# Attention inside a fused four-layer kernel: projections moved to a block's first step, closing weight sums behind them, one addition for four heads

## The chip, the cores and the metric

The kernel runs on one core of a Trainium2 chip. The metric is the device time of one execution in microseconds; the time given for a kernel is the median over several executions. All data are fp32.

## What is computed

Four layers run in a row on x, 16 images of 384 channels and 16x16 points, seen as two sequences of N = 2048 tokens. The change touches only the first, an attention with 12 heads of 32 dimensions whose values are the input itself:

```
qk   = (xt @ qk_w.T)                          # q and k, 12 heads of 32
attn = softmax(q * 32**-0.5 @ k.T)
attn = alpha * eye + beta * attn - gamma / N
out  = attn @ v                               # v = xt
```

The other three are a ConvNeXt block (7x7 depthwise convolution, norm over channels, 384 to 1536 to 384, with a global response norm between the two products), a Sobel block (two fixed 3x3 filters, a 768 to 384 product, norm, gelu, residual) and a block with two 1x1 convolutions round a 3x3 depthwise one, a linear attention, and a norm with an MLP of 384 to 1536 to 384.

## The kernel before, in words

**Attention.** There are six units (2 sequences times 3 groups of four heads). A unit has 4 blocks of 512 queries, a block 16 steps of 128 keys; 24 blocks and 384 steps in all. A step `t` of block `n` issues, in this order:

- `scores(n, t)`: four score products, one for each head, on TensorE (`st` in the profile) into two PSUM tiles, each two banks wide, of a pool of three; then two exponentials on ScalarE, each 128x1024 (two heads), into two `e` tiles in SBUF (a pool of eight, so four steps deep).
- `weighted` of the step before: four products with the values (`av`), added up over the block in one PSUM bank, and on VectorE the running sum of the `e` tiles, in two additions of 128x1024 (`s`). After `ADDS[n]` steps such a sum ends and a new one begins: the list has 4, 8, 16 or 2 for each of the 24 blocks.
- A finished sum is added up over the partitions by TensorE with a matrix of ones (`weights`, `dn` in the profile). A sum that ends inside the block does so in four quarters of 128 columns in later steps; the one that ends the block in one piece of 512 columns, two steps later. Then `finish` copies the result to SBUF (`r`), and VectorE inverts it in four pieces, scales the `av` sum with it (copied before to `va` by ScalarE, beside `xg`, the part with `alpha` and `gamma`) and writes the layer's output, one piece in each following step.
- In step `SLOT` = 5 of a block, `project` makes two of the coming q or k tiles: 12 matmul instructions (`p`) into the third PSUM tile, two copies on ScalarE, and on the way a load of v by SyncE's queue. There are projections in blocks 0 to 21 (a single one in block 21).
- `fill` puts work of the second layer into the step: taps of the 7x7 convolution on VectorE (`y`), and, from block 20 on, the norms of its first tiles (the leads). How much comes from `pace`, a table of what a step takes on TensorE and on VectorE.

The three engines' instructions are pinned to this program order. A dictionary `due` holds what is to be issued in which step.

**Everything after attention** is laid out by a list scheduler (`Plan`), which takes, of the operations that can start within `SLACK`, that of the task with the lowest rank. `TURNS` is the order of the 16 MLPs (0 for the second layer, 1 for the fourth; one weight set is loaded for each entry), `RANK` the ranks, `AFTER` the point from which convolution outputs may use buffers of another pool. Only the first two convolution tiles may be made during attention.

A group's line in the profile is always L96, a helper that records every instruction, so the tiles' names tell what is meant.

Of the kernel before, what the change touches and what calls it, by code (L numbers as in the profile page):

```python
# [9 lines left out]
F32 = mybir.dt.float32  # L10
AF = mybir.ActivationFunctionType
ALU = mybir.AluOpType
# [3 lines left out]
P = 128  # L16
C = 384
NC = C // P
NB = 2
# [4 lines left out]
HD = 32  # L24
# [3 lines left out]
BLK = 512  # L28
NBLK = N // BLK
NIP = NBLK  # L30
NQC = N // P
SLOT = 5
LEAD = 20 * NQC + 6
FIRST = NQC + 10

TURNS = (
    (0, ((0, 0), (0, 1), (0, 2), (0, 3),)),
    (1, ((0, 0), (0, 1),)),
    (0, ((1, 0), (1, 2),)),
    (1, ((0, 2),)),  # L40
    (0, ((1, 1), (1, 3),)),
    (1, ((1, 0), (0, 3), (1, 2), (1, 1), (1, 3),)),
)
AFTER = ('x4', 0, 2)

RANK = {
    "mid": ((36.6, 22.0, 24.3, 85.6), (18.6, 42.9, 96.6, 26.9)),
    "l1": ((50.1, 89.5, 75.2, 4.0), (51.1, 16.8, 81.7, 28.5)),
    "l3c": ((45.7, 99.2, 100.9, 121.0), (-20.9, -6.3, 70.9, 62.0)),
    "conv": 109.4,  # L50
}
SLACK = 0.196
JUNK = 2

ADDS = (16, 8, 16, 16, 4, 4, 4, 2, 2, 8, 16, 16, 4, 16, 2, 4, 16, 8, 4, 4, 4, 4, 4, 4)
XB, YB, SB = 12, 2, 22
TB = BLK // P
RB = 2 * HW
# [135 lines left out]
def pace(t):  # L194


    n, i = divmod(t - 1, NQC)
    adds = ADDS[n]
    pe, dve = 2.066, 2.275 if t and i % adds else 0.0
    at = i - adds - 1  # L200
    parts = sum(j * adds // 4 == at % adds for j in range(4)) if at >= 0 else 0
    if parts:
        pe += 0.22 * parts
    elif i == 1 and n > 0:
        pe += 0.87
    else:
        pe += 0.09
    if n > 0:
        dve += {2: 0.88, 3: 0.88, 4: 0.88, 5: 0.88, 6: 0.6, 7: 0.66}.get(i, 0.0)
    return pe, dve  # L210


# [185 lines left out]
def attention(tc, X, xt, L0, block, small, col, cols, ones, load_qk, banks, fill, bound):  # L398
# [6 lines left out]
    with ExitStack() as actx:  # L405
        pool = lambda name, bufs, **kw: actx.enter_context(tc.tile_pool(name=name, bufs=bufs, **kw))
        wqk_sb = pool("wqp", 1).tile([P, NC, 2, NC, P], F32, name="wqk_sb")
        load_qk(wqk_sb)
        ep = pool("ep", 8)
        sp = pool("sp", 4)  # L410
        op = pool("op", 2)
        pst = pool("pst", 3, space=PSUM)
        pacc = pool("pacc", 1, space=PSUM)
# [37 lines left out]
            return made, early, late  # L451


        due = {}

        def unit(u, made, gm):

            b, g = units[u]
            q, keys, v = made["q"], made["k"], made["v"]
            adds = ADDS[u * NBLK : (u + 1) * NBLK]  # L460
            acc, sums = {}, {}

            def scores(n, t):
                es = []
                for i in range(2):
                    es.append(ep.tile([P, 2, BLK], F32, tag="e", name=f"e_{u}_{n}_{t}_{i}"))
                sts = [bank2(f"st_{u}_{n}_{t}_{i}") for i in range(2)]
                for h in range(4):
                    rows = slice(HD * h, HD * (h + 1))
                    pe.matmul(  # L470
                        sts[h // 2][:, h % 2, :],
                        keys[t // TB][rows, ts(t % TB, P)],
                        q[n][rows, :],
                        start=True,
                        stop=True,
                    )
                for i in range(2):
                    act.activation(es[i], sts[i], AF.Exp, scale=HD**-0.5)
                return es

            def weighted(n, t, es):
                if t == 0:
                    acc["av"] = pacc.tile([P, BLK], F32, tag="av", name=f"av_{u}_{n}")
                for h in range(4):
                    pe.matmul(
                        acc["av"][HD * h : HD * (h + 1), :],
                        v[t // TB][:, (t % TB) * P + HD * h : (t % TB) * P + HD * (h + 1)],
                        es[h // 2][:, h % 2, :],
                        start=(t == 0),
                        stop=(t == NQC - 1),  # L490
                    )
                at = t % adds[n]
                for i in range(2):
                    if at == 0:
                        sums[i] = es[i]
                    elif at == 1:
                        s = sp.tile([P, 2, BLK], F32, tag="s", name=f"s_{u}_{n}_{t}_{i}")
                        dve.tensor_tensor(s, sums[i], es[i], ALU.add)
                        sums[i] = s
                    else:  # L500
                        dve.tensor_tensor(sums[i], sums[i], es[i], ALU.add)


                k = (u * NBLK + n) * NQC + t
                if at == adds[n] - 1:
                    parts = 1 if t == NQC - 1 else 4
                    for i in range(parts):
                        due.setdefault(k + 2 + i * adds[n] // 4, []).append(
                            lambda i=i, summed=dict(sums): weights(
                                n, t, summed, ts(i, BLK // parts)  # L510
                            )
                        )
                for f in due.pop(k, ()):
                    f()
                if t == NQC - 1:
                    va = op.tile([P, BLK], F32, tag="va", name=f"va_{u}_{n}")
                    act.activation(va, acc["av"], AF.Copy, scale=1.0)
                    xg = op.tile([P, BLK], F32, tag="xg", name=f"xg_{u}_{n}")
                    act.activation(
                        xg, X[b][n][:, g, :], AF.Identity, scale=col("alpha", g), bias=gm  # L520
                    )
                    due[k + 2].append(lambda: finish(n, va, xg))

            def weights(n, t, summed, at):
                if t == adds[n] - 1 and at.start == 0:
                    acc["dn"] = pacc.tile([P, BLK], F32, tag="dn", name=f"dn_{u}_{n}")
                for h in range(4):
                    pe.matmul(
                        acc["dn"][HD * h : HD * (h + 1), at],
                        ones[:, :HD],  # L530
                        summed[h // 2][:, h % 2, at],
                        start=(t == adds[n] - 1 and at.start == 0),
                        stop=(t == NQC - 1),
                    )

            def finish(n, va, xg):

                if g == 0:
                    L0[b][n] = block(f"l0_{b}_{n}")
                k = u * NBLK + n  # L540
                r = op.tile([P, BLK], F32, tag="r", name=f"r_{u}_{n}")
                act.activation(r, acc["dn"], AF.Identity, accum_out=bound[:, 0, k : k + 1])

                def invert(i):
                    dve.reciprocal(r[:, ts(i, P)], r[:, ts(i, P)])

                def scale():
                    dve.tensor_tensor(va, va, r, ALU.mult)

                def check():  # L550
                    junk = op.tile([P, BLK], F32, tag="junk", name=f"junk_{u}_{n}", bufs=1)
                    act.activation(junk, r, AF.Identity, accum_out=bound[:, 1, k : k + 1])

                def put():
                    dve.scalar_tensor_tensor(
                        L0[b][n][:, g, :], va, col("beta", g), xg, ALU.mult, ALU.add
                    )

                todo = [*(lambda i=i: invert(i) for i in range(TB)), scale, put]
                for i, f in [*enumerate(todo), (8, check)]:  # L560
                    due.setdefault((k + 1) * NQC + 2 + i, []).append(f)

            return scores, weighted

# [14 lines left out]
        for u, (b, g) in enumerate(units):  # L579
            steps = late_steps  # L580
            scores, weighted = unit(u, made, means[b][0][:, g : g + 1])
            if u + 1 < len(units):
                made, early, late_steps = projections(*units[u + 1])
                steps = steps + early
            for n in range(NBLK):
                for t in range(NQC):
                    es = scores(n, t)
                    added = 0.0
                    if before:
                        before()  # L590
                    before = lambda f=weighted, a=(n, t, es): f(*a)
                    if t == SLOT and steps:
                        added = project(f"p_{u}_{n}", steps[:2])
                        del steps[:2]
                    fill((u * NBLK + n) * NQC + t, added)
            assert not steps
        before()
# [7 lines left out]
def conv_seq_kernel(  # L605
# [869 lines left out]
    if fast:  # L1475
# [5 lines left out]
        def fill(t, added=0.0):  # L1481
# [12 lines left out]
            for task in (*leads, conv):  # L1494
# [3 lines left out]
                while task is not conv or ("y", 0, YB - 1, NC - 1) not in plan.made:  # L1498
                    op = task.head
# [1 line left out]
                        task.rest = t + 1 + (before.engine == "DVE")  # L1501
                        break
                    if op.engine == "DVE":
                        if free < max(0.4, op.length - 1.5):
                            break
                        free -= op.length + 0.12 * (before in op.after)
                    if not plan.holds(task, "wa") or not plan.step(task):
# [144 lines left out]
```

## Time and profile before

| what | value |
|---|---|
| median of 3 runs | 2674.13 us (2673.81 to 2677.04) |
| profiled execution | 2679.38 us, its span 2677.6 us |
| attention in it, first score product to the last step | 22.1 to about 1048.5 us |
| TensorE busy | 2644.6 us, 99% of the span |
| VectorE busy | 2011.5 us, 75% |
| ScalarE busy | 1557.5 us, 58% |
| DMA | 55.69 MB, 21 GB/s on average |

The profiled execution is 5.25 us longer than the median, and has 1.8 us outside its span. In the groups a row gives line, engine, operation, output and inputs, their shapes, the count, busy time and mean duration, and idle time before it with what ended it. PE is TensorE, DVE VectorE, ACT ScalarE. One matmul of the source is two instructions in the profile, so a step's four score products are eight `st` instructions. Ends of matmuls are modelled and overlap the next; the distance between starts is what a step really takes.

### The profile page before, as it was taken

To read this page: it belongs to the slowest core of one execution; us is meant where nothing else is said; L and a number is where in the kernel's file an instruction comes from. 1 tells how busy PE (TensorE), PEld (TensorE's weight loads), DVE (VectorE), ACT (ScalarE), POOL (GpSimd) and SP (SyncE) were. 2 spreads that over 40 slices of the span, in tenths; PEclk is the share of its full clock that TensorE was granted. 3 is DMA by queue.
4 is the path that set the end of the run, shared out by engine and by line. 5 is a ranking of instruction groups with operands and counts; after the bars stand their busy time and mean duration, and the time that the engine had idled before them with its cause. 6 is when DMAs were issued, how large, how long until landed. Compare 5 with 4: busy or idle time off the path is not lost. (4 is left out here: it accounts for less than half of the span.)

```text
span 2677.6 us, 32803 instructions
## 1 busy us (share of the span) xinstructions
PE 2644.6 (99%) x12997; PEld 1061.5 (40%) x12997; DVE 2011.5 (75%) x2588; ACT 1557.5 (58%) x2314; POOL 7.4 (0%) x54
## 2 busy tenths in 40 slices
PE   8999999999999999899999999999999999999999
PEld 2223333233323323345444454444444444454443
DVE  5999999999999889999999999999652202732300
ACT  6787878878787888564565335457443542625201
POOL 0000000000000000000000000000000000000000
PEclk9999999999999999999999999999999999999999
DMA  3000000000000003000001001011001110000000
GB/s 150 5 13 1 9 9 5 13 1 5 13 1 1 1 13 108 23 0 0 1 1 47 25 12 31 29 36 36 24 24 36 47 36 24 0 1 1 12 17 20
DMA packets 28851, 55.69 MB, mean 21 GB/s; under 512 B 1680, under 2 KB 14096, under 8 KB 28688
## 3 DMA queue, kind: packets, MB, share of 16 engines
q1 hardware_dynamic: 28544, 53.35, 6.0%
q8 instruction: 104, 1.70, 0.3%
q14 instruction: 59, 0.48, 0.1%
q10 hardware_dynamic: 144, 0.15, 0.0%
HBM read 47.21 MB, written 6.29 MB: 20 GB/s over the span
## 5 line engine op out<-in xcount | busy, mean ns | idle before, releaser
L96 ACT ACTIVATE e<-st 128x1024 f32<-128x1024 f32 x768 | 743.2, 1025 | 88.5 <-PE st L96 80.7
L96 DVE SCALAR_TENSOR_TENSOR y<-l,vec,y 128x420 f32<-128x420 f32 (+8 forms) x1152 | 660.0, 638 | 5.0
L96 DVE TENSOR_TENSOR s<-s,e 128x1024 f32<-128x1024 f32 x444 | 513.3, 1216 | 11.7 <-ACT e L96 11.2
L96 PE MATMUL st<-q,k 32*128 32x512 f32 x3072 | 474.1, 641 | 4.0 <-ACT e L96 2.3
L96 PE MATMUL av<-e,v 128*32 128x512 f32 x3072 | 410.9, 606 | 4.3 <-ACT va L96 4.2
L96 PE MATMUL ph_l<-y,wa 128*128 128x512 f32 x576 | 261.4, 597 | 0.0
L96 PE MATMUL ph_l3c<-d_l3c,wa 128*128 128x512 f32 x576 | 258.4, 593 | 0.0
L96 PE MATMUL po_l<-hid_l,wb 128*128 128x512 f32 x576 | 255.7, 596 | 1.1 <-ACT hid_l L96 1.1
L96 PE MATMUL po_l3c<-hid_l3c,wb 128*128 128x512 f32 x576 | 256.6, 593 | 0.0
L96 PEld LDWEIGHTS st<-q,k 32*128 32x128 f32 x3072 | 146.1, 183 | 220.1 <-issue 132.4
L96 DVE TENSOR_TENSOR s<-e,e 128x1024 f32<-128x1024 f32 x162 | 191.0, 1221 | 54.7 <-ACT e L96 36.0
L96 ACT ACTIVATE hid_l<-ph_l,vec 128x512 f32<-128x512 f32 x96 | 66.0, 687 | 202.9 <-PE ph_l L96 202.8
L96 ACT ACTIVATE hid_l3c<-ph_l3c,vec 128x512 f32<-128x512 f32 x96 | 65.6, 687 | 202.6 <-PE ph_l3c L96 202.5
L96 PEld LDWEIGHTS av<-e,v 128*32 128x32 f32 x3072 | 60.6, 108 | 298.1 <-issue 274.0
L96 DVE SCALAR_TENSOR_TENSOR o_l3c<-po_l3c,vec,l 128x512 f32<-128x512 f32 x24 | 17.5, 748 | 209.6 <-PE po_l3c L96 208.8
L96 PEld LDWEIGHTS po_l<-hid_l,wb 128*128 128x128 f32 x576 | 109.5, 191 | 139.1 <-issue 128.0
L96 PEld LDWEIGHTS ph_l3c<-d_l3c,wa 128*128 128x128 f32 x576 | 108.8, 190 | 137.2 <-issue 133.4
L96 PEld LDWEIGHTS ph_l<-y,wa 128*128 128x128 f32 x576 | 109.1, 191 | 136.0 <-issue 125.1
L96 PEld LDWEIGHTS po_l3c<-hid_l3c,wb 128*128 128x128 f32 x576 | 109.0, 190 | 134.6 <-issue 132.8
L96 PE MATMUL p<-x,wqk_sb 128*128 128x512 f32 x288 | 132.3, 610 | 1.2 <-DMA x<-in_x_dram 1.2
L96 DVE SCALAR_TENSOR_TENSOR g_l3a<-h_l3a,dw,g_l3a 128x450 f32<-128x450 f32 (+1 forms) x192 | 119.0, 702 | 4.2 <-ACT g_l3a L96 4.1
L96 PEld LDWEIGHTS dn<-s,ones 128*32 128x32 f32 x2016 | 64.1, 110 | 125.4 <-issue 107.0
(155 smaller groups left out, 2446.3 us busy)
## 6 DMA issues: line engine op xcount, KB each, us to landing
wa<-in_w_dram SPq DMA_DIRECT2D x9, 768.0 KB, 4.5
wb<-in_w_dram SPq DMA_DIRECT2D x9, 768.0 KB, 5.0
wa<-in_mlp_w_dram SPq DMA_DIRECT2D x9, 768.0 KB, 4.4
wb<-in_mlp_w_dram SPq DMA_DIRECT2D x9, 768.0 KB, 4.5
x<-in_x_dram SPq DMA_DIRECT2D x8, 768.0 KB, 10.6
v<-in_xt_dram SPq DMA_DIRECT2D x24, 256.0 KB, 2.7
out_dram<-o_l3c SPq DMA_DIRECT2D x24, 256.0 KB, 2.1
qkv<-in_qkv_wT_dram SPq DMA_DIRECT2D x3, 576.0 KB, 11.1
```

The source lines that it names most:

```text
L96: self.last = self.tc.keep_in_program_order(make(*args, **kw))
```

## The change

Six things change together.

1. `project` is called in step 0 of a block in place of step 5.
2. For blocks 0 to 20 (those below `PAIRED` = 21, whose next block begins with a projection) the closing weight sum and `finish` go into a list `behind` that is emptied right after that projection. The inversions, scaling and output then begin with the next block's step 0, where they began with step 2. Blocks 21 to 23 keep the old places.
3. One `e` tile holds four heads (pool of four) and one addition of 128x2048 takes the place of two of 128x1024; the `s` pool goes from four to two.
4. `ADDS` goes from 7 blocks with 16, 3 with 8, 11 with 4 and 3 with 2 to 3 with 16, 4 with 8 and 17 with 4. Quarters that would fall into the next block are issued in the block's last step.
5. `pace` follows these places, and in `fill` a VectorE operation that gives a PSUM bank back is issued whatever time is left in the step.
6. `TURNS` has four entries in place of six; `RANK`, `SLACK` and `AFTER` have other values.

```diff
-SLOT = 5
+PAIRED = (NB * NC - 1) * NBLK + 1
 TURNS = (
     (0, ((0, 0), (0, 1), (0, 2), (0, 3),)),
-    (1, ((0, 0), (0, 1),)),
-    (0, ((1, 0), (1, 2),)),
-    (1, ((0, 2),)),
-    (0, ((1, 1), (1, 3),)),
-    (1, ((1, 0), (0, 3), (1, 2), (1, 1), (1, 3),)),
+    (1, ((0, 0), (0, 1), (0, 2),)),
+    (0, ((1, 0), (1, 1), (1, 3), (1, 2),)),
+    (1, ((0, 3), (1, 0), (1, 3), (1, 1), (1, 2),)),
 )
-AFTER = ('x4', 0, 2)
+AFTER = ('x4', 0, 1)
...
-SLACK = 0.196
+SLACK = 0.134
...
-ADDS = (16, 8, 16, 16, 4, 4, 4, 2, 2, 8, 16, 16, 4, 16, 2, 4, 16, 8, 4, 4, 4, 4, 4, 4)
+ADDS = (16, 4, 4, 16, 8, 4, 4, 4, 16, 4, 8, 8, 4, 4, 4, 4, 8, 4, 4, 4, 4, 4, 4, 4)
...
-    pe, dve = 2.066, 2.275 if t and i % adds else 0.0
+    pe, dve = 2.066, 2.2 if t and i % adds else 0.0
...
-        ep = pool("ep", 8)
-        sp = pool("sp", 4)
+        ep = pool("ep", 4)
+        sp = pool("sp", 2)
...
-                    act.activation(es[i], sts[i], AF.Exp, scale=HD**-0.5)
+                    act.activation(
+                        es[:, 2 * i : 2 * (i + 1), :], sts[i], AF.Exp, scale=HD**-0.5
+                    )
...
+                    dve.tensor_tensor(acc["sum"], acc["sum"], es, ALU.add)
...
+                        if end and block < PAIRED:
+                            behind.append(f)
+                        else:
+                            when = k + 2 + i * adds[n] // 4
+                            due.setdefault(
+                                when if end else min(when, (block + 1) * NQC - 1), []
+                            ).append(f)
...
-                    due[k + 2].append(lambda: finish(n, va, xg))
+                    (behind if block < PAIRED else due[k + 2]).append(
+                        lambda: finish(n, va, xg)
+                    )
...
+                first = (k + 1) * NQC + (0 if k < PAIRED else 2)
                 for i, f in [*enumerate(todo), (8, check)]:
-                    due.setdefault((k + 1) * NQC + 2 + i, []).append(f)
+                    due.setdefault(first + i, []).append(f)
...
-                    if t == SLOT and steps:
+                    if t == 0 and steps:
                         added = project(f"p_{u}_{n}", steps[:2])
                         del steps[:2]
+                    for f in behind:
+                        f()
+                    behind.clear()
...
-                        if free < max(0.4, op.length - 1.5):
+                        bank = any(tag == "mm" for tag, _ in op.gives)
+                        if free < max(0.4, op.length - 1.5) and not bank:
                             break
```

## Prediction

> **What bounds the kernel now.** I read the page first: engines, then groups.
>
> ```profile
> PE 2644.6 (99%) x12997; PEld 1061.5 (40%) x12997; DVE 2011.5 (75%) x2588; ACT 1557.5 (58%) x2314; POOL 7.4 (0%) x54
> L96 DVE TENSOR_TENSOR s<-s,e 128x1024 f32<-128x1024 f32 x444 | 513.3, 1216 | 11.7 <-ACT e L96 11.2
> L96 DVE TENSOR_TENSOR s<-e,e 128x1024 f32<-128x1024 f32 x162 | 191.0, 1221 | 54.7 <-ACT e L96 36.0 <-PE dn L96 18.4
> ```
>
> PE never rests, so no other engine's busy time counts for itself: only PE's own work, its waits, and matmuls that take longer than they need. Next the windows (columns: time, PE, PEld, DVE, ACT, POOL, granted clock, DMA).
>
> ```profile
> 22.00:938.00 916.00, 909.99 (x7415) 283.91 (x7414) 861.01 (x915) 741.16 (x882) 0.00 (x0) 1.00 0.03 8
> 1080.00:1100.00 20.00, 12.28 (x23) 4.88 (x22) 16.95 (x30) 14.35 (x32) 0.00 (x0) 0.76 0.00 0
> 1480.00:1876.00 396.00, 395.73 (x1061) 181.97 (x1060) 388.86 (x607) 190.73 (x343) 2.25 (x16) 1.00 0.09 28
> 1876.00:2278.00 402.00, 402.00 (x1142) 185.51 (x1141) 131.82 (x169) 164.35 (x309) 1.15 (x8) 1.00 0.10 32
> ```
>
> Attention runs PE, DVE (94%) and ACT (81%) all nearly full. Right after it there is a hole: PE idles 7.7 us in 20, and the clock falls to 0.76. From 1480 on PE is full, though DVE is at 98% until 1876. PE's waits name the hole:
>
> ```profile
> PE av L96 <- ACT va L96: 4.2, 16, 0.3
> PE su_l L96 <- DVE s_l L96: 3.6, 1, 3.6
> PE sv_l L96 <- DVE gmean_l L96: 2.1, 1, 2.1
> PE pg_l L96 <- DVE gs_l L96: 1.9, 1, 1.9
> ```
>
> Idle time isn't all: inside attention PE loses time that counts as busy. The timeline of PE at a block's beginning (start, length, what; step 1 begins at 148.61):
>
> ```profile
> 148.61 1.31 PE L96 MATMUL st<-q,k 32*128 32x512 f32 x8
> 150.20 1.07 PE L96 MATMUL av<-e,v 128*32 128x512 f32 x8 [0.28 <-ACT va L96]
> 151.19 1.74 PE L96 MATMUL st<-q,k 32*128 32x512 f32 x8
> 152.86 1.07 PE L96 MATMUL av<-e,v 128*32 128x512 f32 x8
> 153.75 1.04 PE L96 MATMUL dn<-s,ones 128*32 128x512 f32 x8
> 154.72 1.14 PE L96 MATMUL st<-q,k 32*128 32x512 f32 x8
> 155.79 1.07 PE L96 MATMUL av<-e,v 128*32 128x512 f32 x8
> ```
>
> and ACT beside it:
>
> ```profile
> 149.54 0.61 ACT L96 ACTIVATE va<-av 128x512 f32<-128x512 f32 x1
> 150.01 0.83 ACT L96 ACTIVATE xg<-x,gm,vec 128x512 f32<-128x512 f32 x1
> 150.72 3.77 ACT L96 ACTIVATE e<-st 128x1024 f32<-128x1024 f32 x4
> 154.85 0.60 ACT L96 ACTIVATE r<-dn 128x512 f32<-128x512 f32 x1 [0.36 <-PE dn L96]
> ```
>
> An undisturbed step is 2.066 us from st to st (1.07 and 0.996). Step 1 takes 2.58, step 2 takes 3.53 where 2.066 + 0.858 for the 512-column dn would do: 1.12 us lost. ACT is behind for `va` and `xg`, 1.2 us between exponentials; the next score products wait for PSUM tiles, and av for `va`. From the starts in the PE timeline I summed this over blocks 1 to 21: 16.4 us, 0.78 for a block.
>
> [...] the st at 151.19 counts 1.74 busy for work of 1.07. [...] av takes 0.996 before st, 0.883 before dn of its own mode, so a change costs about 0.11. [...] the window with the 3.65 us wait shows 0.76.
>
> **The change part by part.** Unit prices from starts in the timeline: a projection of two tiles 5.35, a quarter dn 0.219, a closing dn 0.858 behind av.
>
> *Projection to step 0.* It removes nothing from PE (22 calls, as before; SyncE's v loads and the two ACT copies move with it, five steps earlier in the block, each with blocks of lead, and SP's queue has nothing due behind them). But `va` and `xg` now run while PE projects: after the exponentials of step 0, ACT has 3 us free and needs 1.3. The av wait and the late exponentials go. What is late next: at the projection's end T come two copies (1.0) and `r` (0.7), so exponentials of step 1 begin at T + 1.8, where st of step 1, behind dn, ends at T + 2.05. The exponentials end near T + 3.9, av of step 1 is due at T + 4.1. Just covered; I leave 0.25 us a block for it. Gain 21 x (0.78 - 0.25) = **-11.1**. In block 0 the gap between the first st and av (5.14 us for what should be 3.14) falls behind the projection too: **-2**, less likely.
>
> *Closing dn behind the projection.* Same dn, but reached from the 128x128 mode: at worst a mode change more each, 0.11 x 21 = **+2.4**; at best 0. The trace has no p followed by dn; I take the worst. The sum it reads: the last addition begins with av of step 15, 2.2 us, and the projection lasts 5.35, so dn won't wait.
>
> *Quarters.* Counted from `ADDS`: 81 sums before, 79 after, 24 of them closing; quarters 228 to 220: -8 x 0.219 = **-1.8**. Steps without quarters also wobble: in blocks with 16, every second step takes 2.24 instead of 2.07, because the two exponentials barely fit. Behind step 5 that costs 1.07 us in a block with 16, 0.9 with 8, 0.12 with 4. Over blocks 1 to 21 the old list loses 12.3 us including two waits for `y` of 1 us; with the new mix 14 x 0.12 + 4 x 0.9 + 2 x 1.07 = 7.4: **-4.9**.
>
> *One addition for four heads.* [...] Successive additions start 1.134 apart in the trace, so 0.08 overlaps: 2.21 against 2.27 a pair. 303 pairs become 305 additions: 688 to 674 us, **14 us of DVE** freed, on PE nothing by itself. The single addition starts 0.9 us later, having to wait for both exponentials; av may have to as well. The `e` ring is four steps deep: an exponential may start about 4 us after the addition that frees its buffer could begin. With the inversions (0.86 each) in steps 0 to 3, scaling 0.6, output 0.66 and additions of 2.2 against PE's 2.07, DVE falls some 2 to 3 us behind by step 6. A block with 4 recovers at steps 4, 8, 12, where nothing is added; one with 16 keeps 2 to 3 us of lag and may lose about 1 us. Bounds for this part: 0 to +7; I take 0 beside the 0.25 above.
>
> *Behind attention.* 33 taps of the second convolution tile, 22 us of DVE, are left when attention ends, and this tile's norm is what `su_l` waits for at 1089, when the first MLP's matmuls are used up. With 14 us of taps moved forward the tile is ready about that much sooner. The 7.7 us hole goes, and with it the lost clock, 0.24 x 20 = 4.8. The global norm's own waits (pg_l, sv_l) need a neighbour's matmuls to hide them; I leave 3.5 us. **-9**. Bounds: -12.5 to +10, as a new order from `RANK` and `TURNS` can open other holes; full PE windows after 1350 show only that the old order has none. Weight loads fall from 18 wa and 18 wb to 12 and 12; no PE wait names a DMA after the start, so 0. The last MLP sets the end either way: its tail stays.
>
> *Leads.* Blocks 22 and 23 lose 8.4 us where the norm's square-root table and PSUM tile hold up the exponentials. Two leads instead of one may double it, giving the bank back at once may shrink it: 0, between -4 and +6.
>
> Sum: -11.1 - 2 + 2.4 - 1.8 - 4.9 - 9 = **-26.4**. Against the profiled execution's own 2679.4 that is 2653.0; it stood 5.2 above the median of 2674.1, so the forecast for the median is 2648.
>
> **Rivals.** *A: only attention gains.* The scheduler's new order meets as many holes as the old one: -11.1 + 2.4 - 1.8 - 4.9, some way short of it when DVE is tight: -10 to -17, near 2660. For it: DVE is at 97% for 800 us either way, and attention grown shorter takes back 16 us of DVE's room. Against: 22 us of taps are the named cause of the one big hole.
>
> *B: all stalls go.* Boundaries lose nothing, leads shrink, every PE wait between 1080 and 1350 vanishes: 16.4 + 2 + 1.8 + 6 + 12.5 + 4, less 2.4, is -40: 2634. The waits left in the skeleton of the norms speak against it.
>
> *C: slower, through the `e` ring.* The projection's 5.35 us used to come after three inversions and let DVE catch up; now it comes ahead of them. If DVE is more than 4 us behind by step 5 to 8, exponentials wait for a buffer, PE for them. The price is what DVE is late: at 2 us for each of 21 blocks +42, less the 25 gained, is +17: 2691. It breaks even near 1.25 us a block. By my count the lag stays under 3 us, so the point is not reached, but convolution taps placed too generously by `pace` would carry it there.
>
> *D: no difference.* The gains are eaten by leads and a new hole: within 0.2%, 5.3 us, which is about what a measurement of this kernel can tell from none.
>
> **How the numbers follow.** Forecast (-18 to -34) 0.50, A (-8 to -18) 0.20, B 0.10, D 0.06, C 0.14. Faster 0.80, same 0.06, slower 0.14. The range goes from B's 2634, a little lower, to the median of before: 2632 to 2674. It leaves out most of C and the far end of B.
>
> **What would show it.** Right, if st to st in steps 1 and 2 is 2.1 to 2.3 us, av no longer waits for `va`, the dn behind p takes 0.97 to 1.1, additions 128x2048 last 2.29 us x305, attention ends near 1032, and the wait for `su_l` is gone. Wrong, if ACT's `e` waits for DVE's `s`, if steps 5 to 8 exceed 2.4 us, or if PE idles more than 12 us between 1030 and 1350.

## The result and the profile after

The kernel after takes 2685.32 us (median of 6 runs, 2681.45 to 2685.72) beside 2674.27 us for the kernel before in the same comparison: ratio **1.0033**, 95% interval 1.002 to 1.0046. It is slower by a third of a per cent, where 2648 us were forecast. The runs of each kernel fall into groups at slightly different granted clocks (0.997 to 0.995), mostly near 2674 and 2679 us for before and 2681.5 and 2685.5 for after, which is why the quotient of the two medians, 1.0041, is larger than the ratio; group against group the kernel after is some 7 us slower. The profiled execution took 2685.09 us, its span 2683.3 us, 5.7 more than before's.

First the engines and the additions in the page of the kernel after.

```profile
PE 2644.4 (99%) x12933; PEld 1061.5 (40%) x12933; DVE 2007.2 (75%) x2287; ACT 1568.1 (58%) x2323; POOL 7.5 (0%) x54
L94 DVE TENSOR_TENSOR s<-s,e 128x2048 f32<-128x2048 f32 x226 | 514.5, 2276 | 16.2 <-ACT e L94 1.4
L94 DVE TENSOR_TENSOR s<-e,e 128x2048 f32<-128x2048 f32 x79 | 180.7, 2287 | 36.7 <-ACT e L94 35.9
```

There are 305 additions of 2276 to 2287 ns, as counted. The quarters left out are the 64 PE instructions missing from 12997. The windows (time, PE, PEld, DVE, ACT, POOL, granted clock, DMA):

```profile
22.00:938.00 916.00, 908.83 (x7344) 282.66 (x7346) 869.19 (x667) 742.26 (x881) 0.00 (x0) 1.00 0.03 9
1080.00:1100.00 20.00, 13.81 (x33) 5.64 (x31) 9.38 (x15) 16.57 (x36) 0.00 (x0) 0.92 0.00 0
```

VectorE is busy 869 us in attention's window, against 861 before. That is no relief: 22 more taps of the convolution are done during attention (11 of the second tile are left behind it, where 33 were), and they take more than the additions freed. Behind attention there is a hole again. The clock in this window is better (0.92) only because the stretch at the reduced clock, 1096.7 to 1103.6, lies partly behind it. PE's waits in the kernel after (total, times, longest):

```profile
PE dn L94 <- DVE s L94: 8.2, 8, 1.7
PE po_l L94 <- ACT hid_l L94: 7.6, 2, 4.6
PE pc_l3a L94 <- DVE l L94: 3.6, 1, 3.6
PE su_l L94 <- DVE s_l L94: 1.1, 1, 1.1
```

The waits of `av` for `va` are gone and `su_l` waits 1.1 us in place of 3.6. New is a weight sum `dn` that waits for VectorE's sum; the kernel before has no such wait. `po_l` and `pc_l3a` wait longer than before, where they stood at

```profile
PE po_l L96 <- ACT hid_l L96: 1.1, 2, 0.9
PE pc_l3a L96 <- DVE l L96: 0.8, 1, 0.8
```

PE's timeline at the beginning of block 7, a block with 4 (step 1 begins at 330.22; the part shown of before was the same place in a block with 16):

```profile
329.23 1.06 PE L94 MATMUL dn<-s,ones 128*32 128x512 f32 x8
330.22 1.14 PE L94 MATMUL st<-q,k 32*128 32x512 f32 x8
331.29 1.07 PE L94 MATMUL av<-e,v 128*32 128x512 f32 x8
332.29 1.37 PE L94 MATMUL st<-q,k 32*128 32x512 f32 x8
...
334.58 1.14 PE L94 MATMUL st<-q,k 32*128 32x512 f32 x8
...
336.65 1.31 PE L94 MATMUL st<-q,k 32*128 32x512 f32 x8
...
338.89 1.14 PE L94 MATMUL st<-q,k 32*128 32x512 f32 x8
...
340.96 1.37 PE L94 MATMUL st<-q,k 32*128 32x512 f32 x8
```

Step 1 takes 2.07 us, where it took 2.58. But steps 2, 4 and 6 take 2.29, 2.24 and (its quarter taken off) 2.30 us, each about 0.2 over the bare 2.066.

The span's difference, from starts in the two timelines ("loss" is what steps take above the bare price of their matmuls):

| where | forecast, us | measured, us |
|---|---|---|
| blocks 1 to 21, loss in steps 1 and 2 (16.4 to 4.4) | -11.1 | -12.0 |
| block 0, step 0 | -2 | -2.0 |
| quarters left out | -1.8 | -1.7 |
| change of tiling mode from `p` to `dn` | +2.4 | +2.9 |
| blocks 1 to 21, rest of the loss in step 0 | 0 | +3.5 |
| blocks 1 to 21, loss in steps 3 to 5 | 0 | +1.4 |
| blocks 1 to 21, loss in steps 6 to 15 (12.3 to 17.8) | -4.9 | +5.5 |
| block 0, later steps | 0 | +2.4 |
| blocks 22 and 23 (the leads) | 0 | -0.3 |
| last step to the first `ph_l` | 0 | +1.5 |
| everything after the first `ph_l` (1625.25 to 1629.97) | -9 | +4.7 |
| ahead of the first score product | 0 | -0.2 |

### The profile page after: what moved, and what is told of

Same layout as the page of the kernel before. It is cut to its first block, busy times and chain, and to the rows that moved or that the text cites. A ratio compares the mean times of both kernels' runs of the same rounds, so it can differ in the third digit from the quotient of the medians.

```text
span 2683.3 us, 31719 instructions
## 1 busy us (share of the span) xinstructions
PE 2644.4 (99%) x12933; PEld 1061.5 (40%) x12933; DVE 2007.2 (75%) x2287; ACT 1568.1 (58%) x2323; POOL 7.5 (0%) x54
## 5 line engine op out<-in xcount | busy, mean ns | idle before, releaser
L94 DVE TENSOR_TENSOR s<-s,e 128x2048 f32<-128x2048 f32 x226 | 514.5, 2276 | 16.2 <-ACT e L94 1.4
L94 DVE TENSOR_TENSOR s<-e,e 128x2048 f32<-128x2048 f32 x79 | 180.7, 2287 | 36.7 <-ACT e L94 35.9
## 6 DMA issues: line engine op xcount, KB each, us to landing
x<-in_x_dram SPq DMA_DIRECT2D x8, 768.0 KB, 10.4
qkv<-in_qkv_wT_dram SPq DMA_DIRECT2D x3, 576.0 KB, 11.1
```

What stands on the lines that cost most here:

```text
L94: self.last = self.tc.keep_in_program_order(make(*args, **kw))
```

## The experiments

Only ratios from one comparison are set against each other. "Blocks 0 to 20" is the time from the first score product to block 21, "rest" that from the first `ph_l` to the end. Both come from the profiled execution. Kernels with the same attention repeat it closely: blocks 0 to 20 differ by 0.05 us between after and e1, by 0.26 between before and e2. Except in e8, no clock was reduced in blocks 0 to 20.

| kernel | ratio to before | interval | blocks 0 to 20, us | rest, us |
|---|---|---|---|---|
| before | 1 | | 901.90 | 1625.25 |
| after | 1.0033 | 1.002 to 1.0046 | 902.11 | 1629.97 |
| e1_old_order | 1.0057 | 1.0041 to 1.0074 | 902.06 | 1640.98 |
| e2_new_order | 1.0143 | 1.0126 to 1.016 | 901.64 | 1663.07 |
| e4_proj | 1.0144 | 1.0127 to 1.0161 | 901.03 | 1656.72 |
| e5_four | 1.0078 | 1.0062 to 1.0095 | 903.40 | 1643.56 |
| e6_late | 1.0034 | 1.0022 to 1.0047 | 901.88 | 1630.55 |
| e7_new_adds | (one run, 2679.53 us) | | 895.51 | 1625.90 |
| e8_split | 1.0023 | 1.0013 to 1.0032 | 905.88 | 1629.93 |
| e9_no_adds | 0.9996 | 0.9988 to 1.0005 | 894.86 | 1629.77 |
| e11_adds | **0.9977** | 0.9968 to 0.9987 | 896.56 | 1625.12 |
| e12_four | 1.0013 | 1.0006 to 1.0019 | 903.40 | 1626.47 |
| e13_adds_four | 0.9992 | 0.9984 to 1.0001 | 898.29 | 1624.20 |
| e14_old_rest | 1.0019 | 1.0012 to 1.0027 | 900.35 | 1624.03 |
| e15_split_adds | 1.0008 | 1.0000 to 1.0016 | 897.33 | 1631.14 |
| e16_split_old_rest | 0.9996 | 0.9987 to 1.0004 | 896.19 | 1626.26 |

### Which part costs

**e1_old_order**: the kernel after with the old order behind attention.

```diff
-TURNS, AFTER, RANK, SLACK of after
+TURNS, AFTER, RANK, SLACK of before
```

> The changed kernel with the TURNS, RANK, SLACK and AFTER of before. Theory (the new order of the work behind attention costs the 6 us lost there, attention itself gains nothing): attention as in the changed kernel, 1031.5 us from first st to first ph, and the rest near the 1625 of before, so a time near 2679. Rival (what attention leaves behind, more taps done and DVE's sums late, opens the holes whatever the order): the rest stays at 1630 or more, time 2684 or above.

The rest became 11 us longer, not shorter, and the whole took 2693.73 us. That the new order is simply worse is refuted.

**e2_new_order**: the kernel before with the new order.

```diff
-TURNS, AFTER, RANK, SLACK of before
+TURNS, AFTER, RANK, SLACK of after
```

> The kernel before with only the new TURNS, RANK, SLACK and AFTER. Theory (order costs 6 us): attention unchanged at 1030.3 us from first st to first ph, the rest near 1631, time near 2680. Rival (order is not to blame): 2674, within 2 us.

The rest took 1663 us, which neither reading had expected. The two largest new waits of PE in this kernel are

```profile
PE pd_l3a L94 <- DVE g_l3a L94: 15.2, 1, 15.2
PE pg_l L94 <- DVE gs_l L94: 12.2, 2, 10.2
```

Together with e1: the old order with the old taps left over takes 1625 us, the new with the new 1630, the old with the new 1641, and the new with the old 1663. What attention leaves undone (33 taps of the second convolution tile before, 11 after) and the order behind it belong together. A run that moves the number of taps therefore says little by its total. Attention has to be read by itself, or with taps and order held fixed.

**e4_proj**: the kernel before with parts 1 and 2 alone, and with what follows from them for late quarters, `pace` and `fill`.

```diff
+ due, behind = {}, []         # closing dn and finish behind the projection
...
-                    if t == SLOT and steps:
+                    if t == 0 and steps:
```

> The kernel before with projections in step 0 and the closing sums behind them alone: two e tiles and two additions per step, ADDS and order of before. Theory (steps 1 and 2 gain 12 us, but PE gives it back later in the block, where ACT has no pause any more and sums of DVE come late, whatever the form of the addition): attention between 1027 and 1034, PE waits of dn for DVE s in blocks with 8 and 16. Rival (the single addition of four heads is what makes the sums late): attention near 1020, no such waits.

Blocks 0 to 20 took 0.9 us less than before, although steps 1 and 2 there lost 4.3 instead of 16.4 us. First score product to first `ph_l` took 1035.1 us, a little over the theory's range. The total says nothing on the part (other taps: `pf_l` waited 13.1 us behind attention). So even with the old additions the 12 us nearly all go elsewhere in the block: step 0 loses 8.5 instead of 1.3 and steps 6 to 15 lose 20 instead of 12.

**e5_four**: the kernel before with part 3 alone, `pace` at 2.2.

```diff
-    dve.tensor_tensor(sums[i], sums[i], es[i], ALU.add)            # twice
+    dve.tensor_tensor(acc["sum"], acc["sum"], es, ALU.add)         # 128x2048
...
-    pe, dve = 2.066, 2.275 if t and i % adds else 0.0
+    pe, dve = 2.066, 2.2 if t and i % adds else 0.0
```

> The kernel before with only the four-head e tile and the one addition (places, ADDS and order of before; pace counts 2.2 for it). Theory: attention within 2 us of 1030.3, since DVE's gain of 0.06 us a step is not PE's. Rival (coarser waits on the one tile slow every step): attention 1036 or more, st and av longer in plain steps.

Blocks 0 to 20 took 1.5 us more. First score product to first `ph_l` took 1033.4 us, between the two readings. The rest suffered from the other number of taps.

**e7_new_adds**: the kernel before with the new `ADDS` alone, one run.

```diff
-ADDS = (16, 8, 16, 16, 4, 4, 4, 2, 2, 8, 16, 16, 4, 16, 2, 4, 16, 8, 4, 4, 4, 4, 4, 4)
+ADDS = (16, 4, 4, 16, 8, 4, 4, 4, 16, 4, 8, 8, 4, 4, 4, 4, 8, 4, 4, 4, 4, 4, 4, 4)
```

> The kernel before with only the new ADDS list. Only attention is read, as the work behind it is laid out anew. Theory (more blocks with 4 give fewer plain steps and 8 fewer quarters, so the list alone gains): from first st to first ph 1024 instead of 1030.3. Rival (the list gains nothing in itself): 1029 or more.

Blocks 0 to 20 were 6.4 us shorter. The span that the expectation named was not (1029.6 us, which by its words is the rival's), nor was the whole: 45 taps were left behind attention, a lead had not been finished in it, and PE waited at the first MLP:

```profile
PE ph_l L96 <- ACT y L96: 13.1, 1, 13.1
```

The next three runs set the first number in `pace` so that taps and order behind attention are exactly those of before.

**e11_adds**: the list alone, with `pace` at 2.21.

```diff
-ADDS = (16, 8, 16, 16, 4, 4, 4, 2, 2, 8, 16, 16, 4, 16, 2, 4, 16, 8, 4, 4, 4, 4, 4, 4)
+ADDS = (16, 4, 4, 16, 8, 4, 4, 4, 16, 4, 8, 8, 4, 4, 4, 4, 8, 4, 4, 4, 4, 4, 4, 4)
-    pe, dve = 2.066, 2.275 if t and i % adds else 0.0
+    pe, dve = 2.066, 2.21 if t and i % adds else 0.0
```

> The kernel before with the new ADDS, and 2.21 in place of 2.275 as pace's price of a step's additions, so that as many taps are done in attention as before and the work behind attention is laid out exactly as before. Theory (the new list alone gains the 6.9 us in blocks 0 to 21 that it gained without the taps): 6.9 us less than before, 2667 where before is 2674. Rival (it gained only because VectorE had fewer taps to do): no difference, within 2 us.

2671.08 us beside 2678.7: 0.9977, **the fastest of all, and faster than both kernels**. First score product to the last step is 6.8 us shorter than before; the granted clock inside attention was reduced for less time, worth 1.7 us of that. Blocks 0 to 20, where neither trace shows a reduced clock, are 5.3 us shorter. How much of it a single execution shows depends on the clock: the lowest times of the two kernels, both at a granted clock of 0.997, lie 3.1 us apart (2670.81 and 2673.95).

**e12_four**: part 3 alone, with taps and order as before (`pace` at 2.275). The edit of the addition is that of e5.

> The kernel before with the four-head e tile and the one addition; pace keeps 2.275, so that taps and the work behind attention are exactly those of before. Theory (the one addition begins and ends later, so the closing sum and the inversions hold up steps 1 and 2): blocks 0 to 21 2 us slower, time 2 us above before. Rival (the 2.3 us lost with it so far came from the extra taps): equal or faster than before.

1.0013, blocks 0 to 20 again +1.5 us: the four-head addition is a loss by itself.

**e13_adds_four**: both, `pace` at 2.21.

> The change without its projections: new ADDS, four-head e tile and one addition, projections in step 5 and closing sums in their old places, and the order of before; pace counts 2.21, with which the work behind attention is laid out exactly as before. Theory (the parts add up): -6.9 + 2.3 = -4.6 us against before. Rival (they don't): -7 or better.

Blocks 0 to 20: -3.6 us. The parts add up (-5.3 and +1.5).

**e14_old_rest**: the kernel after's attention with the old order and, by `pace`, the old number of taps behind it.

```diff
-TURNS, AFTER, RANK, SLACK of after
+TURNS, AFTER, RANK, SLACK of before
-    pe, dve = 2.066, 2.2 if t and i % adds else 0.0
+    pe, dve = 2.066, 2.26 if t and i % adds else 0.0
```

> The change's whole attention, but with the order of before, and 2.26 as pace's price, with which as many taps are done and the work behind attention is laid out exactly as before. Theory (attention itself gains nothing, and the changed kernel's loss is in what its order makes of the work behind): blocks 0 to 21 within 1.5 us of before, first ph 1 to 1.5 us later after the last step, time 1 to 2 us above before. Rival (attention's tail costs the rest something in any case): 5 us or more above before.

1.0019. The rest is 1624 us, but attention up to its last step is 3.2 us longer than before's: blocks 0 to 20 save 1.55 us and blocks 21 to 23 lose 4.8, where a lead's stall has moved into block 21 (up to 1.7 of it because the clock was reduced for longer). Beside e13, moving the projections on top of the other two parts makes blocks 0 to 20 2.05 us longer (3.8 with the kernel after's own taps).

### Where the gain at a block's beginning goes

**e9_no_adds**: the kernel after leaves out every addition but the first of each sum, so that VectorE has about 515 us less to do.

```diff
-                else:
-                    dve.tensor_tensor(acc["sum"], acc["sum"], es, ALU.add)
```

> The changed kernel that leaves out all additions but the first of each weight sum, so VectorE has some 490 us less to do in attention. Theory (late sums come from VectorE, the loss of 0.17 to 0.23 us in every second plain step from ScalarE and the three PSUM tiles): the 8.2 us of dn waiting for s and what they drag along go, plain steps stay, attention near 1022. Rival (VectorE being behind is also what slows plain steps, through the e buffers): nearly all of the 45 us above the bare steps goes, attention below 1005.

First score product to first `ph_l`: 1023.01 us, 8.5 less than the kernel after. No `dn` waits for a sum any more. So up to 8.5 us belong to VectorE's additions. The rhythm of the following steps stays as it was, seen in PE's timeline of this kernel in the same block:

```profile
332.12 1.37 PE L94 MATMUL st<-q,k 32*128 32x512 f32 x8
...
334.42 1.14 PE L94 MATMUL st<-q,k 32*128 32x512 f32 x8
...
336.49 1.37 PE L94 MATMUL st<-q,k 32*128 32x512 f32 x8
```

The score products of steps 2 and 4 again take 1.37 where 1.14 is the rule. What delays them is not VectorE's additions.

**e6_late**: the kernel after with each quarter one step later.

```diff
-                            when = k + 2 + i * adds[n] // 4
+                            when = k + (2 if end else 3) + i * adds[n] // 4
```

> The changed kernel with each quarter of a weight sum one step later (still at latest in the block's last step); the work behind attention is the same. Theory (in the four blocks with 8 the first quarter comes before VectorE has the sum; each such wait costs 1.1 to 1.3 us with what it drags along): attention 1027 us instead of 1031.5 from first st to first ph, 4 fewer PE waits of dn for DVE s, time 4 us less than the changed kernel's. Rival (the lateness is only handed on): within 1 us of the changed kernel.

1.0034, nothing gained. `dn` waited 5.8 us instead of 8.2, in 4 places instead of 8. The four waits of quarters went, but steps 6 to 15 together lose 0.5 us more than in the kernel after, and attention's last `dn` waits 2.7 us in place of 1.7. The delay was handed on rather than removed.

**e8_split**: the kernel after with one projected tile in step 0 and the other in step 6.

```diff
-                    if t == 0 and steps:
-                        added = project(f"p_{u}_{n}", steps[:2])
-                        del steps[:2]
+                    if t in (0, 6) and steps:
+                        added = project(f"p_{u}_{n}_{t}", steps[:1])
+                        del steps[:1]
```

> The changed kernel with one projection in step 0 and the other in step 6 of a block in place of both in step 0. Theory (steps without other PE work lose 0.17 to 0.23 us every second one until a pause in ScalarE's load resets them; a projection of 2.8 us in step 6 is such a pause): steps 6 to 15 of blocks 1 to 21 lose 12 us instead of 17.8, the second entry into the 128x128 mode costs 21 x 0.23 = 4.8, so attention within 2 us of 1031.5. Rival (the pause has nothing to do with it): the 4.8 comes on top, attention 1036.

1.0023. Blocks 0 to 20 became 3.8 us longer, since one tile's 2.8 us no longer cover the last addition (step 0 loses 13.0 us instead of 7.8; `dn` waits 7.3 us in 4 places). The longest of these waits, 3.4 us in block 1, came with 6.8 us at half the clock, in which PE was busy for 6.2, so an estimated 3 us of the 3.8 are the clock's. For the second entry into `p`, taken at 0.23 us, the kernel after shows 0.20 (2.77 us for the single tile in block 21, 5.35 for two). In steps 6 to 15 the loss is 20.1 us instead of 17.8, although no quarter waits there any more (3.4 us in the kernel after), and a block with 4 loses 0.33 us in step 6 instead of 0.23. So the expectation that a pause in step 6 would take most of the rhythm away was not met. That attention came out within its range all the same (1031.0 us to the first `ph_l`) is owed to blocks 22 and 23, which lose 6.2 us less here and were not part of the argument.

### The long addition

In block 3, which adds up all 16 steps in one sum, the timelines of the kernel after show ScalarE, VectorE and PE at the end of the block:

```profile
188.50 1.94 ACT L94 ACTIVATE e<-st 128x1024 f32<-128x1024 f32 x2 [0.46 <-DVE s L94]
190.89 1.94 ACT L94 ACTIVATE e<-st 128x1024 f32<-128x1024 f32 x2 [0.46 <-DVE s L94]
```

```profile
183.71 16.67 DVE L94 TENSOR_TENSOR s<-s,e 128x2048 f32<-128x2048 f32 x7
```

```profile
194.02 5.42 PE L94 MATMUL p<-x,wqk_sb 128*128 128x512 f32 x12
200.44 1.07 PE L94 MATMUL dn<-s,ones 128*32 128x512 f32 x8 [1.00 <-DVE s L94]
201.43 1.14 PE L94 MATMUL st<-q,k 32*128 32x512 f32 x8
```

Seven additions of 2.29 us take 16.67: they start (16.67 - 2.29)/6 = **2.40 us** apart. In the whole trace 139 such pairs start 2.396 apart, with 0.104 us idle between them, though operands are there. Before, two chains took turns:

```profile
143.70 8.04 DVE L96 TENSOR_TENSOR s<-s,e 128x1024 f32<-128x1024 f32 x7
```

(8.04 - 1.22)/6 = 1.137 apart, 2.27 a step. With PE at 2.066 a step, VectorE now falls back 0.33 us a step instead of 0.2. By the end of the block the `e` ring is full, ScalarE waits 0.46 a step, and PE runs at VectorE's pace: 2.40. A whole projection of 5.4 us is not long enough to cover what is left, and the closing `dn` waits 1.00 more.

Two readings were open: each addition reads the sum that the one before it wrote, or the coarse four-head tile comes free too late. The trace of the kernel after speaks for the first, where a sum ends in block 4 and a new one begins:

```profile
219.26 4.68 DVE L94 TENSOR_TENSOR s<-s,e 128x2048 f32<-128x2048 f32 x2
223.85 2.28 DVE L94 TENSOR_TENSOR s<-e,e 128x2048 f32<-128x2048 f32 x1
226.24 2.29 DVE L94 TENSOR_TENSOR s<-s,e 128x2048 f32<-128x2048 f32 x1
```

The first two start 2.39 apart (4.68 less the 2.29 of one), and the fourth starts 2.39 behind the third. But the third, which begins a new sum and reads nothing that the second wrote, starts 2.21 behind it (at 223.85, the second at 221.65), at the same size. This happens four times in the trace, at 2.21 each time.

**e15_split_adds**: the kernel after, tiles of four heads as they are, each addition split into its two halves.

```diff
...
-                    dve.tensor_tensor(acc["sum"], acc["sum"], es, ALU.add)
+                    for i in range(2):
+                        half = slice(2 * i, 2 * (i + 1))
+                        dve.tensor_tensor(
+                            acc["sum"][:, half, :], acc["sum"][:, half, :], es[:, half, :], ALU.add
+                        )
```

> The kernel after, with two additions of 128x1024 on the two halves of the same four-head tiles in place of one of 128x2048; nothing else differs, so the list of sums, the taps and the order behind attention are the kernel after's. Theory (each long addition reads the sum that the one before it has written and starts 2.396 us behind it; two alternating halves start 1.135 apart, 2.27 a pair): in block 3 the waits of ScalarE's e for VectorE's s (0.46 a step) go or fall under 0.2, the closing dn waits under 0.5 there, all waits of dn for s fall from 8.2 to under 5 us, and blocks 0 to 20 take 1 to 4 us less than 902.1; the whole 2681 to 2684, ratio 1.0015 to 1.003. Rival (the four-head tile itself is what costs: a buffer comes free only when both halves are added): waits and blocks as in the kernel after within 0.7 us, ratio 1.003 to 1.004.

1.0008, and blocks 0 to 20 4.8 us shorter, more than expected. The end of block 3 in VectorE's and ScalarE's timeline, and the waits of `dn`:

```profile
176.85 20.52 DVE L94 TENSOR_TENSOR s<-s,e 128x1024 f32<-128x1024 f32 x18
```

```profile
186.82 4.01 ACT L94 ACTIVATE e<-st 128x1024 f32<-128x1024 f32 x4 [0.30 <-PE st L94]
```

```profile
PE dn L94 <- DVE s L94: 2.2, 4, 0.7
```

(20.52 - 1.21)/17 = 1.136 apart again. ScalarE waits for PE, not for VectorE, and `dn` waits 2.2 us instead of 8.2: only the four quarters are left. It is the single chain, not the tile.

**e16_split_old_rest**: the same split in e14's kernel.

> The same split of the addition in the kernel that has the new attention, the old order and the old number of taps behind it (blocks 0 to 20 were 900.35 there, the whole 1.0019). Theory: blocks 0 to 20 1 to 4 us shorter, ratio 1.0003 to 1.0015, with the stall of the leads in blocks 21 to 23 left as it was. Rival: within 0.7 us of 900.35, ratio near 1.002. If it is under 0.9977 the split version with all three parts beats the one with the new list of sums alone.

0.9996 where e14 had 1.0019; blocks 0 to 20 4.2 us shorter. With the chain split, all three parts come back to the kernel before, but not to e11: the stall of a lead in block 21 remains (blocks 21 to 23 take 124.0 us, 121.0 in e11), and blocks 0 to 20 are the same within 0.4 us. The moved projections thus bring nothing on top of the new list.

## Why the prediction was wrong

The forecast was 26.4 us off the span; it grew by 5.7. Of the 32.1 us between them, 15.2 lie behind attention (the last two losses of the table taken together), 10.4 in steps 6 to 15, and 7.3 in places put at nothing: step 0, steps 3 to 5 and block 0. The local signs that the prediction named for being right mostly came (steps 1 and 2, `va`, the `dn` behind `p`, the additions); they watch places and not the total. Point by point, by the prediction's steps:

**Projection to step 0, -11.1: the saving is real (-12.0), but it was counted as net.** `av` no longer waits for `va`, and steps 1 and 2 take what was forecast, to 0.9 us. "Just covered" held as well, for `av` of step 1. What was missed is the score products of step 2. During the projection ScalarE stands idle for 3.7 us and cannot work ahead, since PE makes no scores meanwhile:

```profile
324.37 0.61 ACT L94 ACTIVATE va<-av 128x512 f32<-128x512 f32 x1
324.85 0.82 ACT L94 ACTIVATE xg<-x,gm,vec 128x512 f32<-128x512 f32 x1
329.33 1.07 ACT L94 COPY k<-p 128x512 f32<-128x512 f32 x2 [3.66 <-PE p L94]
330.36 0.60 ACT L94 ACTIVATE r<-dn 128x512 f32<-128x512 f32 x1
331.45 3.94 ACT L94 ACTIVATE e<-st 128x1024 f32<-128x1024 f32 x4 [0.41 <-PE st L94]
```

It then starts on step 1's exponentials when that step's scores end, with nothing in hand. Four exponentials take 3.94 us against PE's 4.13 for two steps, so it gains only 0.1 us a step, and until it has done so every second step's scores come up against an occupied PSUM tile. The trace names what they wait for: in steps 2, 4 and 6 of this block the third score instruction starts 0.24, 0.18 and 0.24 us after the first, where 0.01 is the rule, and each time 0.05 us after the first exponential of the step before has ended. A typical block with 4 loses 0.23, 0.17 and 0.23 us in steps 2, 4 and 6. It loses another 0.15 in step 11, behind a copy of `r` on ScalarE in step 10 (0.84 us), which stood in step 12 before and cost 0.11 there. Together that is 0.78, which is what steps 1 and 2 lost on average before; of these, step 4's 0.17 and most of step 11's had been lost before too. e9 shows that VectorE's additions aren't the cause. That a fourth tile or shorter exponentials would end it is not shown by a run.

**Closing dn behind the projection, +2.4: right in size for the mode change, wrong on the wait.** The mode is the tile that the profile gives with a matmul: 128*128 for `p`, 128*32 for `av` and `dn`. `dn` behind p starts 0.996 us before the next scores against the 0.858 taken, 0.14 a block, 2.9 in all. But "dn won't wait" failed: it assumed that the last addition begins with `av` of step 15. In the three blocks with 16 VectorE is so late by then that the projection's 5.4 us don't cover it, and the closing `dn` waits 1.00 to 1.08 us. That is 3.1 of the 3.5 us in step 0. The last one of attention, which has no projection ahead of it, waits 1.67. In each of the four blocks with 8, a quarter also came before its sum was done:

```profile
223.99 0.43 PE L94 MATMUL dn<-s,ones 128*32 128x128 f32 x8 [0.91 <-DVE s L94]
```

These eight waits make the 8.2 us. The quarters' 3.4 lie in the row for steps 6 to 15.

**Quarters, -1.8: right (-1.7). The wobble of steps 6 to 15, -4.9: wrong, +5.5.** The new list does roughly what was said where projections stay in step 5: e11 loses 8.95 us there, before 12.3, forecast 7.4 (the sum has 14 blocks with 4 where blocks 1 to 21 hold 15, which is 0.1 us). The term applied losses measured behind a projection in step 5 to blocks whose projection is in step 0. ScalarE's catching up now reaches into step 6, so that a block with 4 loses 0.38 us in steps 6 and 11, and not 0.12. This is the largest miss in attention: 10.4 us, 3.4 of it the waits of quarters.

**One addition for four heads, 0 with 14 us of VectorE freed: wrong.** The step that failed is "2.21 against 2.27 us a pair". The overlap of 0.08 us was measured between *alternating* chains and carried over to a single chain. There it is 0.104 us of idle time instead: 2.396, so VectorE's pace is 0.13 us slower per step and not 0.06 faster. That one addition of 128x2048 lasts 2.29 us, from which the 2.21 starts, no trace of before showed; the kernel after's shows 2276 to 2287 ns. It is the distance between two that was wrong, and the trace of before had shown it, though not on this sum. The norms add three tiles of squares into one, each addition reading what the one before it wrote:

```profile
1333.73 1.48 DVE L96 TENSOR_TENSOR s_l3c<-s_l3c,s_l3c 128x512 f32<-128x512 f32 x2
```

One takes 0.69, so the second starts 0.79 behind the first, with the same 0.104 us of idle time. The kernel's own `fill` charges an operation for this too:

```python
free -= op.length + 0.12 * (before in op.after)
```

Undone by itself (e15) this step is worth 4.6 us up to the first `ph_l`: 1.8 in step 0, 1.4 in block 0, 0.7 in the later steps, 0.9 between the last step and `ph_l`, less 0.3 in the leads. Its bounds of 0 to +7 did hold it; the value taken was at the wrong end.

**Behind attention, -9: wrong, +1.5 and +4.7.** The gain was counted too high to begin with: the 4.8 us for the clock are half of all the time at the reduced clock, idle time included, and PE was busy for 6.2 us of it, so by estimate 3.1 were to be had (at half the clock eight `av` took 1.94 us, at 976.5 in before, where 1.07 is the rule). The named wait did shrink: `su_l` waits 1.1 us, and 20 us earlier. What the prediction bounded at +10 and then left out took its place. PE's timeline of the kernel after:

```profile
1067.55 1.13 PE L94 MATMUL su_l<-s_l,ones 128*128 128x512 f32 x2 [1.07 <-DVE s_l L94]
...
1093.31 1.12 PE L94 MATMUL ph_l<-y,wa 128*128 128x512 f32 x2 [0.97 <-ACT y L94]
1095.15 0.35 PE L94 MATMUL pg_l<-gs_l,ones 128*128 128x2 f32 x2 [0.71 <-DVE gs_l L94]
1100.12 32.86 PE L94 MATMUL po_l<-hid_l,wb 128*128 128x512 f32 x72 [4.62 <-ACT hid_l L94]
...
1182.64 4.24 PE L94 MATMUL pc_l3a<-l,ca 128*128 128x512 f32 x6 [3.55 <-DVE l L94]
```

The global response norm is a chain through all engines between the first MLP's two products. Before, PE waited 1.93 and 2.13 us in it and had `sv_l` to do. Now it has no other matmuls ready, and waits 4.62. PE's idle time from the first `ph_l` to its last matmul grew from 12.6 to 16.1 us. The time for which PE was busy at half the clock grew as well, from 9.6 to 12.0 us, and half of that difference, 1.2, was lost by the same estimate. Together, 3.5 and 1.2 us account for the 4.7, to within some tenths. The 1.5 us ahead of it is the last closing `dn`, 1.67 us late. With the addition split (e15) that wait is gone, and 0.9 of the 1.5 with it. e1 and e2 show why the part could not be read from before: each of the two orders does worse with the other's leftover taps. Whether another order for the new number reaches 1624 us stays open; no run searched for one.

**Leads, 0**: right (-0.3) with the kernel after's taps. The table of the square root is seen in the trace of before as two loads of 1.28 us on ScalarE (at 970.13 and 972.13, round `s_l`), and PE's `st` waits 0.83 and 1.21 us there. In e14 and e16 the stall moved into block 21: blocks 21 to 23 take 4.8 us more than before in e14, and 2.9 more than e11 in e16.

**The rivals.** C had a mechanism that occurs ("exponentials wait for a buffer"), and two of its three signs came: `e` waits for `s`, and PE idles 17.1 us between 1030 and 1350 (11.8 before). The third came by its letter only: step 6 of a block with 4 takes 2.52 us with its quarter, 2.30 without. But C put it down to the projection ahead of the inversions, at 2 us in each of 21 blocks. Where `e` waits for `s` in block 3, it is the single chain's pace, and undoing the chain everywhere is worth 4.6 us. A was right that the new order meets as many holes as the old, but took attention's gains as sure. A forecast of 0.14 for slower left out that three of the gains rested on one assumption: VectorE and ScalarE no later than before at each place to which work was moved.

## What to carry over

A stall at a place where an engine is behind doesn't vanish when the place is cleared: ask what stock of finished work the engine starts the next stretch with, and follow it until it has caught up. Two half-size accumulations that take turns can be faster than one of full size (here 2.27 us a step against 2.40), so before merging instructions that depend on themselves, look for the distance between starts of a *dependent* pair, not of any pair; another part of the same trace may hold one, as the norms did here. And where a hand-fitted order follows a stage that fills its slack with later work, hold what is left over fixed before reading a change's total; here the list of sums alone, with leftovers held, was 0.23% faster than before, which the whole change buried.

## What the runs showed of the hardware

- An fp32 addition of 128x2048 on VectorE that reads what the one before it wrote starts 2.396 us after it (139 pairs, after). An independent instruction behind an addition starts after 2.14 to 2.21 us, an independent addition of the same size after 2.21. Halves of 128x1024 on two sums in turn start 1.136 apart (e15).
- `dn` in tiles of 128x32 behind products of 128x128 costs 0.14 us more than behind `av`, whose tiles are 128x32 too (0.996 in after, 0.858 in before).
- The granted clock fell to 0.50 at PE waits of different lengths: in the kernel before for 10.2 us behind a wait of 3.65, with two more of 1.93 and 2.13 in it (at 1090), for 3.4 us behind one of 1.51 (at 1288), and for 6.8 us at two of 0.83 and 1.21 (at 974); in the kernel after for 6.8 us at a wait of 2.97 (at 1332). What sets it off, no run shows.
